# Four-layer graph network on one core: a quarter of a clamp's columns goes from GpSimd to VectorE in thirty groups of layer 2, and four degree sums go from layer 0 to layer 1

## The chip, the cores and the metric

The kernel runs on one core of a Trainium2 chip, as one launch. The metric is the device time of the launch in microseconds (us). PE is the matrix engine (TensorE; PEld is its weight load), DVE is VectorE, ACT is ScalarE, POOL is GpSimd, and SP is the engine whose queue issues the loads from memory.

## The reference, cut to what matters

There are 4096 nodes with 64 features each. The matrix `adj` has 4096 x 4096 floats (64 MB)[...], so every layer reads it again. Each of the four layers normalises `x`, computes a graph layer of the result and adds it to `x`.

```python
# layer 0: plain sum over neighbours
h = relu(layernorm(x));  x = x + relu((adj @ h) @ W.T + b)
# layer 1: hyperbolic attention
h, q, k = lorentz_linear(...)               # q and k from h
att = adj * sigmoid((2 + 2 * (qm @ k.T)) / att_scale + att_bias)
s = att @ h;  x = x + s / sqrt(clip(abs(lorentz_norm(s)), 1e-08))
# layer 2: log map between all pairs of nodes, weighted with adj / degree
deg = maximum(adj.sum(axis=1, keepdims=True), 1e-08)
log_ij = logmap(x[:, None], x[None, :])     # needs arctanh of a distance per pair
agg = einsum('ij,ijc->ic', adj / deg, log_ij)
x = x + expmap(0, agg @ weight + bias)
# layer 3: weights that decay with the rank of a neighbour, from a cumsum of the mask
x = x + w(rank) @ (h @ weight) + bias
```

Two things matter here. The degree `deg` is used only in layer 2, but it needs a sum over the whole of `adj`, which the kernel takes while earlier layers pass over it. And the distance of a pair in layer 2 is the same both ways, so it is computed once for a pair of nodes and used for both directions.

## The kernel before, in words

**Tiles.** `adj` is laid out so that one load brings a group: a tile of 128 x 2 x 512 floats (512 KB), for one row `ib` of 512 target nodes (eight rows, NB) and two chunks of 128 source nodes (sixteen groups `g` in a row, NG). Loads are issued by SP in a fixed order (`feed`, L804 to L813) into ten buffers: six of `adjp` and four of `adj01`, the latter in layers 0 and 1 only. A buffer can be loaded again when all users of its group are done with it (`left` counts them): PE for the sums, and DVE as well where it takes a degree sum.

**Order of the work.** The kernel is written as many threads (`l0_sums`, `l2_clamps`, ...), each of which says on which engine its next step runs and when its inputs are ready. `in_turn` (L733) always takes the thread that can start first by a cost model, `Pace` (L60), and emits its instruction; the order of each engine's instructions is then fixed at compile time. All instructions are issued by one helper, `InOrder` (L124), so the profile shows the line L132 for nearly everything, and groups are told apart by the names of their tiles. Threads joined by `in_steps` (L1266) run in a fixed order relative to each other: the second number of each entry says by how many steps a stage lies behind. Where `Pace` expects PE to wait 0.6 us or more, `keep_warm` (L768) puts idle matmuls of the identity with itself (`tr<-ident`) on PE.

**Layer 0.** For each group PE adds adj x h into an accumulator (`pair_sum`, L866), four passes in f32. DVE adds the group into `dg` (`degree_sums`, L890), a running sum of 128 x 2 x 512; the first group of a row is a copy. At the end of a row `after0` (L566) copies the accumulator, adds the two halves of `dg`, and PE turns `dg` into degrees by matmuls with a column of ones. In rows 1 to 6 the groups in `LEFT` (3, 7, 11, 15) are left out of this sum; they are added up in layer 1 instead, and `after1` (L591) then has four more matmuls with ones, a copy to `r_c` on ACT and an addition to `deg` on DVE. In row 0 and row 7 all sixteen groups are summed in layer 0. The last twelve groups of layer 0 alternate with the first of layer 1 (`EARLY`), and layer 1's rows 0 and 1 are run together at the start.

**Layer 1.** PE makes q k for a group (`mm<-qT,kT`), ACT the sigmoid (`sig<-mm`), DVE multiplies by `adj` (`sig<-sig,adj`), PE sums (`acc<-sig,HL`).

**Layer 2.** The work is a list of 72 groups, `work`: row `ib`, and for each column block `J` from `ib` on two halves. A group with J = ib has only pairs within one block: its first half is whole, and its second is "cut" to half of its columns. A group with J > ib is a "two": its result is used directly for row `ib` and also, transposed, for row `J`. One step for one group runs through all engines:

- PE: the product of a pair (`mm<-RT,LT` and `mm<-RB,LB`), transposes (`tr<-ident,t`), the sums `acc<-w,HA` of 128x512 for the row itself (`l2_sums`), and of 128x256 for the transposed half (`l2_sums2`).
- ACT: the square of the product into `v`, then Ln of `v` (`v<-v,minus`), the root (`t<-v`), the inverse (`v<-v`), and the log (`t<-t`).
- POOL: between square and Ln, a clamp of `v` from below, `v<-v`, 128x1024 (`l2_clamps`, L1076 to L1081). It keeps the argument of Ln, v minus a constant, positive.
- DVE: `t<-mm,t` (`l2_coshs`), `t<-t,v` (`l2_pairs`), `w<-t,adj` (`l2_weights`), and two times `w<-tr,adj` 128x512 for the transposed half (`l2_weights2`).

ACT's order in a step is: Ln(k), root(k), square(k+1), inverse(k), log(k). DVE's is: pairs(k-1), weights(k-1), cosh(k), and the two w(k-1). A thread of its own, `l2_gathers` (L1253), adds the finished transposed sums of a column block into `others` after its second half (in row 0 it is a copy on ACT, in later rows an addition on DVE); until that is done, the next block's transposed sums can't start, since they use the same accumulator. At a row's end `after2` (L633) adds `others` to the row's sum (tile `e`) and computes the row's new `x`.

**Layer 3.** Ranks are counted from the mask with bf16 matmuls, made into weights on ACT (`wt<-mm`), and used in two more passes. Nothing in it is touched.

**On POOL** there are, beside the clamps, only small powers (`ln_r<-ln_v`) and constants. In rows of layer 2 the groups of rows' work (`before2`, `after2`) run at the beginning and end of a row, between the steps.

Of the kernel before, what the change touches and what calls it, by code (L numbers as in the profile page):

```python
# [14 lines left out]
ALU = mybir.AluOpType  # L15
# [8 lines left out]
NB = N // W  # L24
CB = W // P
G = 2
NG = NC // G
LEFT = (3, 7, 11, 15)
WAIT = 0.6
EARLY = 12  # L30
BEHIND = NG - CB // G
# [18 lines left out]
B_MIN = 2.0**-22  # L50
SC = 2.0**-19
HALF = 0.25 * SC * SC
Q = 32


# [84 lines left out]
def kernel(ctx: ExitStack, tc: tile.TileContext, a: dict, out: bass.AP):  # L140
# [4 lines left out]
    pace = Pace()  # L145
    PE, DVE, ACT, POOL = (
        InOrder(tc, e, pace, name)
        for e, name in (
            (nc.tensor, "PE"), (nc.vector, "DVE"), (nc.scalar, "ACT"), (nc.gpsimd, "POOL"),
        )  # L150
    )
# [83 lines left out]
    minus = const.tile([P, 1], F32, name="minus")  # L235
    POOL.memset(minus, -HALF)
    shift = const.tile([P, 1], F32, name="shift")
# [3 lines left out]

    rbs = [const.tile([P, CB, 4, Q], F32, name=f"rb{k}") for k in range(2)]
    lbs = [const.tile([P, CB // 2, 4, Q], F32, name=f"lb{k}") for k in range(2)]
    near = const.tile([P, P], BF16, name="near")
    far = const.tile([P, Q], BF16, name="far")
    pick = const.tile([P, KH, Q], BF16, name="pick")
    spread = const.tile([P, 2, 4, NC], BF16, name="spread")

    def later_constants():
# [9 lines left out]
        def weights_of_ranks():  # L259
# [5 lines left out]
            for q in range(4):  # L265
                b = slice(q * Q, (q + 1) * Q)
                DVE.tensor_copy(far[b, :], near_f[b, b])
# [12 lines left out]
            for r in range(4):  # L280
                yield "DVE", lambda: 150.0
                b = slice(r * Q, (r + 1) * Q)
                for h in range(2):
# [63 lines left out]
    def emptied(t):  # L347
        k = [k for k in in_use if k[0] is t][0]
        in_use.remove(k)
        spare.append(k[1])  # L350
# [379 lines left out]
    def latest(*times):  # L730
        return None if None in times else max(times)
# [36 lines left out]
    def keep_warm(wait):  # L768


        if wait < WAIT or not spare or l1[0].get("dist") and "tables" not in opened or "third" in opened:
            return
# [15 lines left out]
    opened = {}  # L788
# [26 lines left out]
    def used(d):  # L815
        d["left"], d["at"] = d["left"] - 1, max(d["at"], pace.latest)

    def ready(t, more=0.0):
        return pace.ready[pace.name(t)] + more

    def arrival(d, more=0.0):
        return ready(d["adj"], more) if "adj" in d else None
# [31 lines left out]


    def group(layer, ib, g):
        degree = (g in LEFT and 0 < ib < NB - 1) == (layer == 1)
        return {"layer": layer, "ib": ib, "g": g, "degree": degree, "left": 1 + degree, "at": 0.0}

    l0 = [group(0, ib, g) for ib in range(NB) for g in range(NG)]
    l1 = [group(1, ib, g) for ib in range(2) for g in range(BEHIND)]
    l1 += [group(1, ib, g) for ib in range(2) for g in range(BEHIND, NG)]
    l1 += [group(1, ib, g) for ib in range(2, NB) for g in range(NG)]
    order = l0[: len(l0) - EARLY] + [d for pair in zip(l0[len(l0) - EARLY :], l1) for d in pair]  # L866
# [109 lines left out]
    def l1_sums():  # L976
        for pair in pairs:
# [24 lines left out]
    work = [  # L1002
        {"ib": i, "J": j, "half": s, "g": j * (CB // G) + s, "first": i == j and s == 0,
         "last": j == NB - 1 and s == CB // G - 1, "two": i < j, "cut": i == j and s == 1,
         "left": 1 + (i == j and s == 1), "at": 0.0}
        for i in range(NB) for j in range(i, NB) for s in range(CB // G)
    ]
    twos = [d for d in work if d["two"]]


    OWN = G * P

    def part(d, t):
        return t[:, :, OWN:] if d["cut"] else t
# [4 lines left out]
    def ago(items, k, n, what):  # L1019

        return items[k - n].get(what) if k >= n else 0.0
# [54 lines left out]
    def l2_clamps():  # L1076
        for d in work:
            yield "POOL", lambda: d.get("square")
            v = part(d, d["v"])
            POOL.tensor_scalar(v, v, HALF * (1.0 + 2.0**-23), None, ALU.max)  # L1080
            d["clamped"] = pace.latest  # L1081

    def l2_signs():
        for d in work:
            yield "PE", lambda: d.get("square")
            for c in range(G):
                b = slice((2 * c + 1) * Q, (2 * c + 1) * Q + 2)
                PE.matmul(
                    part(d, d["ps"])[:, c, :], LB[b, d["g"], :], RB[b, targets(d)],
                    start=False, stop=True, skip_group_check=True,  # L1090
                )
            d["signed"] = pace.latest

    def l2_first_logs():
        for d in work:
            yield "ACT", lambda: latest(d.get("clamped"), opened.get("tables"))
            v = part(d, d["v"])
            ACT.activation(v, v, AF.Ln, bias=minus)
            d["first_log"] = pace.latest
# [19 lines left out]
    def l2_coshs():  # L1119
        for d in work:  # L1120
            yield "DVE", lambda: latest(d.get("root"), d.get("signed"))
            t = part(d, d["t"])
            DVE.scalar_tensor_tensor(t, part(d, d["ps"]), 0.5 * SC, t, ALU.max, ALU.add)
            d["read"] = pace.latest
# [7 lines left out]
    def l2_pairs():  # L1132
        for d in work:
            yield "DVE", lambda: latest(d.get("log"), d.get("inverse"))
            t = part(d, d["t"])
            DVE.scalar_tensor_tensor(t, t, top, part(d, d["v"]), ALU.min, ALU.mult)
            d["paired"] = pace.latest

    def l2_weights():
        for k, d in enumerate(work):  # L1140
            yield "DVE", lambda: latest(
                opened.get("second"), d.get("paired"), arrival(d), ago(work, k, 2, "summed")
            )
            if not d["cut"]:
                d["w"] = w2["pool"].tile([P, G, W], F32, tag="w", name="w")
            DVE.tensor_mul(part(d, d["w"]), part(d, d["t"]), part(d, d["adj"]))
            d["weighed"] = pace.latest
            used(d)
# [34 lines left out]
    def l2_weights2():  # L1183
        k = -1
        for n, d in enumerate(work):
            if d["first"]:
                own = work[n + 1]
                yield "DVE", lambda: latest(
                    ready(d["tr", 0]) if ("tr", 0) in d else None, arrival(own),
                    ago(work, n + 1, 2, "summed"),  # L1190
                )
                own["w"] = w2["pool"].tile([P, G, W], F32, tag="w", name="w")
                DVE.tensor_mul(
                    own["w"][:, :, 0:OWN], d["tr", 0].rearrange("p (k j) -> p k j", j=OWN),
                    own["adj"][:, :, 0:OWN],
                )
                emptied(d["tr", 0])
                used(own)
            k += d["two"]
            for c in range(G if d["two"] else 0):  # L1200
                yield "DVE", lambda: latest(
                    ready(d["tr", c]) if ("tr", c) in d else None,
                    ready(d["adj2"]) if "adj2" in d else None, ago(twos, k, 2, "summed2"),
                )
                if c == 0:
                    d["w2"] = w2["pool"].tile([P, CB, G * P], F32, tag="w2", name="w2")
                j = (d["half"] * G + c) * P
                DVE.tensor_mul(
                    d["w2"][:, :, c * P : (c + 1) * P],
                    d["tr", c].rearrange("p (k j) -> p k j", j=P), d["adj2"][:, :, j : j + P],  # L1210
                )
                emptied(d["tr", c])
            d["weighed2"] = pace.latest
# [242 lines left out]
    def l3_sum():  # L1456
# [22 lines left out]
        if d["last"]:  # L1479
# [10 lines left out]
        ),  # L1490
        in_steps(
            (l2_first_logs(), 0, once), (l2_roots(), 0, once), (l2_squares(), -1, once), (l2_inverses(), 0, once), (l2_logs(), 0, once),
        ),
        l3_counts(),
        in_steps(
            (l2_pairs(), 1, once), (l2_weights(), 1, once),
            (l2_coshs(), 0, once), (l2_weights2(), 1, lambda d: 2 if d["two"] else 1 if d["first"] else 0),
        ),
        l2_clamps(), l2_gathers(), l3_weights(), l3_pass(), l3_masks(), l3_bias(),
        degree_sums(0, l0), degree_sums(1, l1), constants(), *later_constants(),  # L1500
    ])
# [45 lines left out]
```

## Time and profile before

| what | us |
|---|---|
| median of three runs | 1160.33 (1156.4 to 1161.47) |
| profiled execution: its time | 1154.0 |
| profiled execution: span from first to last instruction | 1152.3 |
| granted clock of PE in it | 0.992 of full speed |

| stretch of the span, us | PE busy | DVE busy | ACT busy | POOL busy | GB/s from memory |
|---|---|---|---|---|---|
| 0 to 190 (layer 0) | 168.9 | 164.0 | 77.1 | 47.2 | 371 |
| 190 to 465 (mostly layer 1) | 266.1 | 228.6 | 192.7 | 29.0 | 241 |
| 465 to 911 (layer 2) | 415.3 | 389.8 | 380.3 | 205.1 | 164 |
| 911 to 1152 (mostly layer 3) | 225.7 | 132.0 | 134.9 | 4.4 | 258 |

How to read it: a line of a timeline has the start in us, the duration, the engine, the operation with its output tile, input tiles and shape, the number of instructions joined (x4), and in brackets how long the engine was idle just before and which instruction on which engine ended that. A line of the costliest groups has the total busy time and the mean in ns after the bar, then the idle time just before these instructions and who ended it. In the chain that ended last, each line has the start, the duration and the instruction; "issue" is time for which the profile shows no wait. A line of SP's waits has the engine it waited for, then the total in us, the count and the longest. Matmuls are pipelined, so a busy PE is not PE at its peak.

### The profile page before, as it was taken

The page shows a single profiled execution, that of the slowest core. Times are in us where ns is not written, and L with a number is a line of the kernel's source. Part 1 is how long each engine was busy: PE and PEld are TensorE (multiplying, and loading weights), DVE is VectorE, ACT ScalarE, POOL GpSimd, SP SyncE. Part 2 cuts the span into 40 slices and gives each one's busy share as a digit, 9 for nine tenths or more (in the row PEclk, how much of TensorE's full clock was granted, in tenths as well). Part 3 has the DMA queues.
Part 4 walks back from the last instruction along what each step waited for, and adds up shares of the span by engine and source line. Part 5 has one row for each costly group of instructions (what it writes and reads, how often), then busy time and mean ns, then how long its engine had stood idle before and what let it go on. Part 6 is the DMA issues. An engine that isn't in the chain of part 4 may idle for free.

```text
span 1152.3 us, 15824 instructions
## 1 busy us (share of the span) xinstructions
PE 1076.0 (93%) x5496; PEld 451.4 (39%) x5496; DVE 914.3 (79%) x1473; ACT 785.0 (68%) x1286; POOL 285.7 (25%) x150
## 2 busy tenths in 40 slices
PE   6889999999999999999989989999999889999998
PEld 3234443333333333445434444444444433333332
DVE  7789898778888887697789888898999995555550
ACT  1145546676777667888888888897888664555554
POOL 3022222112100000254445444454445300000000
PEclk9899999999999999999999999999999999999999
DMA  7999999766677677534534535535355489888830
GB/s 277 388 384 395 409 387 357 293 217 204 213 261 241 222 236 249 175 122 161 183 132 168 197 110 186 179 128 187 124 201 173 153 351 369 321 317 321 319 114 10
DMA packets 77192, 271.77 MB, mean 236 GB/s; under 512 B 10040, under 2 KB 11064, under 8 KB 77112
## 3 DMA queue, kind: packets, MB, share of 16 engines
q1 hardware_dynamic: 75456, 270.57, 65.2%
q8 instruction: 43, 0.70, 0.2%
q10 hardware_dynamic: 1656, 0.20, 0.1%
q14 instruction: 37, 0.30, 0.1%
HBM read 269.68 MB, written 1.05 MB: 235 GB/s over the span
## 4 chain that ended last, share of the span: by engine, by line
PE 36%; DVE 18%; issue 17%; ACT 12%; POOL 11%; DMA 5%; ACTq 0%; POOLq 0%; DVEq 0%; SPq 0%
PE acc L132 15%; PE mm L132 13%; POOL v L132 10%; PE tr L132 8%; DMA adj<-in_adjT_dram 4%; ACT wt L132 3%; DVE w L132 2%; DVE sig L132 2%; DVE dg L132 2%; DVE t L132 2%; ACT v L132 2%; ACT sig L132 2%; ACT t L132 1%; DVE r_n L132 1%; POOL ln_r L132 1%
## 5 line engine op out<-in xcount | busy, mean ns | idle before, releaser
L132 PE MATMUL acc<-w,HA 128*65 128x256 f32 (+1 forms) x736 | 245.1, 468 | 15.9 <-DVE w L132 14.2
L132 POOL TENSOR_SCALAR v<-v 128x1024 f32<-128x1024 f32 x72 | 192.7, 2676 | 243.0 <-ACT v L132 238.8
L132 ACT ACTIVATE sig<-mm,att_b,att_a 128x1024 f32<-128x1024 f32 x128 | 148.9, 1200 | 53.7 <-PE mm L132 50.5
L132 ACT ACTIVATE wt<-mm 128x1024 uint16<-128x1024 f32 x124 | 120.2, 1020 | 85.4 <-PE mm L132 85.4
L132 DVE TENSOR_TENSOR sig<-sig,adj 128x1024 f32<-128x1024 f32 x128 | 152.6, 1220 | 28.5 <-ACT sig L132 26.6
L132 DVE TENSOR_TENSOR dg<-dg,adj 128x1024 f32<-128x1024 f32 x114 | 139.2, 1221 | 1.9 <-DMA adj<-in_adjT_dram 0.2
L132 PE MATMUL mm<-qT,kT 64*128 64x512 f32 x512 | 130.5, 623 | 5.9 <-ACT sig L132 5.5
L132 PEld LDWEIGHTS acc<-w,HA 128*65 128x65 f32 x736 | 93.4, 137 | 101.7 <-issue 48.1
L132 PE MATMUL acc<-adj,HA 128*64 128x512 f32 x512 | 123.3, 611 | 9.8 <-DMA adj<-in_adjT_dram 9.7
L132 PE MATMUL acc<-sig,HL 128*64 128x512 f32 x512 | 124.3, 608 | 1.5 <-DVE sig L132 1.4
L132 DVE SCALAR_TENSOR_TENSOR t<-mm,t 128x1024 f32<-128x1024 f32 x72 | 83.6, 1162 | 33.4 <-ACT t L132 24.7
L132 ACT ACTIVATE v<-v,minus 128x1024 f32<-128x1024 f32 x72 | 79.2, 1100 | 44.9 <-POOL v L132 44.4
L132 PE MATMUL acc<-wt,S 128*64 128x512 bf16 x496 | 99.2, 388 | 0.2 <-ACT wt L132 0.2
L132 DVE SCALAR_TENSOR_TENSOR t<-t,v 128x1024 f32<-128x1024 f32 x72 | 83.4, 1159 | 9.6 <-ACT t L132 9.6
L132 DVE TENSOR_TENSOR w<-t,adj 128x1024 f32<-128x1024 f32 x72 | 83.7, 1163 | 1.8
L132 DVE TENSOR_SCALAR RT<-adj 128x1024 bf16<-128x1024 f32 x74 | 51.2, 704 | 40.2 <-PE mm L132 39.1
L132 ACT ACTIVATE t<-t 128x1024 f32<-128x1024 f32 x72 | 72.1, 1001 | 12.4 <-DVE t L132 12.3
L132 PE MATMUL mm<-RT,LT 64*128 64x512 f32 (+1 forms) x288 | 78.5, 622 | 0.0
L132 DVE TENSOR_TENSOR w<-tr,adj 128x512 f32<-128x512 f32 x120 | 77.2, 680 | 0.0
L132 POOL TENSOR_TENSOR ln_r<-ln_v,minus_half 128x4 f32<-128x4 f32 x24 | 41.6, 1731 | 135.0 <-DVE ln_v L132 135.0
L132 ACT ACTIVATE t<-v 128x1024 f32<-128x1024 f32 x72 | 72.8, 1011 | 2.1
L132 PEld LDWEIGHTS mm<-qT,kT 64*128 64x128 f32 x512 | 43.3, 186 | 78.8 <-ACT sig L132 36.1
(214 smaller groups left out, 1407.6 us busy)
## 6 DMA issues: line engine op xcount, KB each, us to landing
adj<-in_adjT_dram SPq DMA_DIRECT2D x512, 512.0 KB, 4.6
x<-in_x_dram SPq DMA_DIRECT2D x4, 256.0 KB, 4.3
out_dram<-h SPq DMA_DIRECT2D x8, 128.0 KB, 2.0
b<-in_b_dram ACTq DMA_DIRECT2D x2, 32.0 KB
W<-in_W_dram ACTq DMA_DIRECT2D x3, 16.0 KB, 5.3
W0T<-in_W0T_dram ACTq DMA_DIRECT2D x2, 16.0 KB, 3.9
W1T<-in_W1T_dram ACTq DMA_DIRECT2D x1, 16.0 KB
W1T<-in_b_dram ACTq DMA_DIRECT2D x1, 0.2 KB
```

What stands on the lines that cost most here:

```text
L132: done = self.tc.keep_in_program_order(getattr(self.engine, op)(*args, **kw))
```

## The change

Two edits.

1. Degree sums. For row 0, the groups 4, 5, 6 and 7 (`FRONT`) are left out of the degree sum of layer 0 and summed in layer 1, as the groups in `LEFT` already are for rows 1 to 6. Row 0 of layer 1 gets a `dg` tile with it: a copy and three additions of 128x1024 on DVE, one addition of its two halves, four matmuls with ones, a copy to `r_c` on ACT and an addition to `deg`.
2. The clamp. A group of layer 2 is "shared" where its row is below 6 and its column block is at least three beyond the row, that is 10, 8, 6, 4 and 2 groups in rows 0 to 4, 30 of 72. For these POOL clamps columns 256 to 1023 (128x768), and DVE clamps columns 0 to 255 (128x256) in a new thread, `l2_clamps_v`, which stands in DVE's fixed order between cosh(k) and the two w(k-1), for group k+1. The Ln of a group then waits for both clamps.

```diff
@@ constants
 LEFT = (3, 7, 11, 15)
+FRONT = (4,5,6,7,)
...
+FLOOR = HALF * (1.0 + 2.0**-23)
+CLAMPED = 256
@@ group
-        degree = (g in LEFT and 0 < ib < NB - 1) == (layer == 1)
+        degree = (g in (LEFT if ib else FRONT) and ib < NB - 1) == (layer == 1)
@@ work
     twos = [d for d in work if d["two"]]
+    for d in work:
+        d["shared"] = d["ib"] < 6 and d["J"] >= d["ib"] + 3 and not d["cut"]
@@ l2_clamps
             yield "POOL", lambda: d.get("square")
-            v = part(d, d["v"])
-            POOL.tensor_scalar(v, v, HALF * (1.0 + 2.0**-23), None, ALU.max)
+            v = part(d, d["v"]) if not d["shared"] else d["v"].rearrange("p c i -> p (c i)")[:, CLAMPED:]
+            POOL.tensor_scalar(v, v, FLOOR, None, ALU.max)
             d["clamped"] = pace.latest
+
+    def l2_clamps_v():
+
+        for d in work:
+            yield "DVE", lambda: d.get("square")
+            if d["shared"]:
+                v = d["v"].rearrange("p c i -> p (c i)")[:, 0:CLAMPED]
+                DVE.tensor_scalar(v, v, FLOOR, None, ALU.max)
+            d["clamped_v"] = pace.latest
@@ l2_first_logs
-            yield "ACT", lambda: latest(d.get("clamped"), opened.get("tables"))
+            yield "ACT", lambda: latest(d.get("clamped"), d.get("clamped_v"), opened.get("tables"))
@@ the list of threads
-            (l2_coshs(), 0, once), (l2_weights2(), 1, lambda d: 2 if d["two"] else 1 if d["first"] else 0),
+            (l2_coshs(), 0, once), (l2_clamps_v(), -1, once), (l2_weights2(), 1, lambda d: 2 if d["two"] else 1 if d["first"] else 0),
```

Because the emission order is chosen by the cost model, the compiled order of each engine also moves. Against before, DVE has 30 clamps of 128x256 more, one copy into `dg` more and one addition less among its sums of groups, and the two small additions at the end of row 0 of layer 1; POOL has 30 clamps of 128x768 in place of 128x1024; PE has four matmuls with ones more, and 62 idle matmuls `tr<-ident` in place of 32 (seven more at the first shared step of each of rows 1 to 4, ahead of the transposed sums of block J = ib + 2, and two more in row 0); ACT has the copy to `r_c`. From the first shared step of a row on, DVE's addition into `others` stands behind `t<-t,v` of the next step, where it stood ahead of it, next to the two `w<-tr,adj`. In row 0 of layer 0 the matmuls of `after0` come one group earlier. The four moved sums stand on DVE behind the last groups of layer 0. SP issues the same 523 transfers in the same order, but the buffers it waits for are freed by PE alone where a degree sum has gone.

## The prediction

> **What bounds the kernel now.** I read the page's chain first, then the costliest groups, then the timelines of one run of equal steps in layer 2, engine by engine, and last the start. In layer 2 the chain that ended last alternates between a clamp on POOL and 3.23 us of other work, so one step takes 6.03 us. The two forms of the clamp are listed by shape.
>
> ```profile
> 624.89 2.76 POOL v L132
> 627.65 3.22 issue
> 630.92 2.77 POOL v L132
> ...
> L132 POOL TENSOR_SCALAR v<-v 128x1024 f32<-128x1024 f32 x64 | 180.4, 2818 | 222.8 <-ACT v L132 218.6 <-DVE w L132 4.2
> L132 POOL TENSOR_SCALAR v<-v 128x512 f32<-128x512 f32 x8 | 12.3, 1540 | 20.2 <-ACT v L132 20.2
> ```
>
> The loop is: clamp(k) on POOL, then on ACT Ln(k), root(k), square(k+1), then clamp(k+1). From start to start ACT takes 1.18 + 0.97 + 1.09 us, the clamp 2.77, the hand-over 0.03: 6.04. While POOL clamps, ACT does inverse and log and then waits 0.99 us for POOL. So a shorter clamp pays until something else takes 6.03 us as well. PE nearly does. The timeline of PE in the same row:
>
> ```profile
> 623.83 1.88 PE L132 MATMUL acc<-w,HA 128*65 128x512 f32 x4
> 625.64 1.13 PE L132 MATMUL mm<-RT,LT 64*128 64x512 f32 x4
> 626.71 0.40 PE L132 MATMUL mm<-RB,LB 32*128 32x512 bf16 x4
> 627.03 1.94 PE L132 MATMUL acc<-w,HA 128*65 128x256 f32 x8
> 628.81 1.04 PE L132 MATMUL tr<-ident,t 128*128 128x128 f32 x8
> 629.68 1.88 PE L132 MATMUL acc<-w,HA 128*65 128x512 f32 x4
> ...
> 639.07 1.94 PE L132 MATMUL acc<-w,HA 128*65 128x256 f32 x8 [0.27 <-DVE w L132]
> ...
> 663.19 1.94 PE L132 MATMUL acc<-w,HA 128*65 128x256 f32 x8 [0.72 <-DVE w L132]
> ...
> 670.41 0.46 PE L132 MATMUL tr<-ident,e 65*128 65x65 f32 x4 [1.31 <-DVE e L132]
> ```
>
> From 623.83 to 629.68 is one step without a wait: 5.85 us. After each row's start PE is behind and runs several steps at 5.85 while ACT and POOL run at 6.03. A step can't get shorter than 5.85, whatever the clamp does; what can be won is PE's waits.
>
> **The clamp.** POOL costs (2.77-1.49)/512 = 2.5 ns a column, so 768 columns take 2.13: 0.64 less. Thirty groups are cut (J at least ib+3: ten, eight, six, four and two in rows 0 to 4). If POOL's loop alone counted, 30 x 0.64 = 19.2 us would go. With PE's 5.85 it is the waits inside the cut stages and at their ends: 0.30+0.30+0.73 in row 0, 0.27+0.30+0.72 in row 1, 0.27+0.73, 0.70, and 0.32 in row 4: 4.6 us. At each row's end PE also waits for e (0.97, three times 1.31, 0.77). With a DVE that is ahead e moves up by about 1.2: today cosh before it waits 0.63 for ACT, and without that DVE is held only by PE's transposes. I take 0.9 + 3 x 1.2 + 0.7 = 5.2.
>
> **VectorE's share.** No row has this operation at 256 columns. A 128x128 TENSOR_SCALAR takes 0.23 and a 128x1024 one 0.68, so 256 columns are 0.30 us by these. DVE's own step is 1.14 (cosh) + 1.19 (two w) + 1.25 + 1.15 = 4.73, and 0.60 more every second step for the sum into "others": with the clamp 5.03 or 5.63, mean 5.33, under 5.85.
>
> But the clamp on DVE starts beside POOL's. The Trainium skill ("SBUF — State Buffer", Who interferes with whom) says that a DVE operation in a 2-port mode and a GpSimd operation exclude each other: the later one blocks until the first one ends. TENSOR_SCALAR from SBUF to SBUF is of that kind. DVE reaches the new instruction 0.2 us after POOL has started, so by the rule it would stand 1.9 us. The trace has both answers:
>
> ```profile
> 593.65 2.76 POOL L132 TENSOR_SCALAR v<-v 128x1024 f32<-128x1024 f32 x1 [3.96 <-ACT v L132]
> 595.71 0.73 DVE L132 TENSOR_SCALAR r_n<-r_n 128x4 f32<-128x4 f32 x1
> ...
> 600.75 2.77 POOL L132 TENSOR_SCALAR v<-v 128x1024 f32<-128x1024 f32 x1 [4.33 <-ACT v L132]
> 602.16 0.17 DVE L132 TENSOR_SCALAR ln_v<-ln_v 128x4 f32<-128x4 f32 x1
> ```
>
> The first came 2.06 us into a clamp and ended with it; the second came 1.41 in and took its usual 0.17. At 513.74 a copy (r_v<-r_i) that came 0.47 us into a clamp took 0.60 instead of 0.15, so it was let go about 0.9 in. So POOL holds DVE at its beginning (to 0.9) and its end (from about 1.9), not between. Scaled to 768 columns: to 0.7 and from 1.4. On time, DVE then stands 0.5 (a step of 5.83 in the mean, still under 5.85); late by that much, not at all. I take 0.5 where DVE is the bound, with 0 and 1.9 as ends.
>
> **Where DVE is the bound: "others".** In the compiled order of the changed kernel the sum into "others" stands behind pairs (t<-t,v), where it stood before or just behind the two w. The sums of the turned half (acc<-w 128x256) wait for it. At the first cut step of rows 1 to 4 DVE has no idle time: in row 1 its cosh ends at 613.08, then clamp 0.3 and 0.5 of standing, two w, pairs 1.25, others 0.60: 616.8 instead of 614.9. PE was there at 615.33 without a wait. It now waits 1.6 us, and this four times: +6.3 (4.9 if DVE never stands; 12.4 if it stands 1.9). The order also has seven idle matmuls at just these places; at 0.13 each (six took 0.94) they lie inside the wait. Two more in row 0 cost 0.3. In later steps others ends as PE arrives, by the same addition, so it costs nothing there. Layer 2: -4.6 - 5.2 + 6.3 + 0.3 = **-3.2 us**.
>
> **The degree sums.** In row 0 of layer 0 DVE sums all sixteen groups, and SP can't load into a buffer that DVE still needs.
>
> ```profile
> SPq L812 <- DVE dg L132: 25.4, 15, 8.8
> ...
> core 0: us, PE busy (x) PEld busy (x) DVE busy (x) ACT busy (x) POOL busy (x), PEclk, DMA share, GB/s
> 24.00:28.00 4.00, 1.08 (x4) 0.20 (x4) 3.87 (x4) 0.00 (x0) 0.00 (x0) 1.00 0.40 135
> ...
> 200.77 0.17 DVE L132 TENSOR_SCALAR lo_n<-lo_n 128x8 f32<-128x8 f32 x1 [2.23 <-ACT lo_sq L132]
> ...
> 201.86 2.36 DVE L132 TENSOR_TENSOR sig<-sig,adj 128x1024 f32<-128x1024 f32 x2 [0.48 <-ACT sig L132]
> ```
>
> The first line is SP's waits up to 80 us; the stretch from 24 to 28 shows DMA at 135 GB/s, against 410 later. Four sums less are 4 x 1.23 = 4.9 us of DVE. Groups 10 and 11 then go into buffers that PE alone frees, at about 16 instead of 18.6 and 20.1. Loads also wait for the load two before them to land, so not all comes through; following the landings group 16 arrives some 3 us sooner. I take -3.5 (ends: -1 and -4.9). No DMA is added or moved in SP's order. The same sums come back behind the last groups of layer 0: a copy and three adds, 0.69 + 3 x 1.22 = 4.4 us on DVE between 191 and 202. DVE's idle 2.23 + 0.48 there covers 2.7; the other 1.7 delay sig, and PE's sums behind it. Row 0 of layer 1 also gets four matmuls with their loads (half of a group of sixteen that took 1.89: 0.9 on a PE that is full), a 0.68 add on DVE and a 0.2 copy on ACT, both in later idle time. Layers 0 and 1: -3.5 + 1.7 + 0.9 = **-0.9 us**.
>
> **Sum.** -3.2 - 0.9 = -4.1 us on the profiled execution (span 1152.3, time 1154.0). That execution lies 6.3 us under the median of the three runs, so the change is put onto the median: 1160.3 - 4.1 = 1156.2.
>
> **Rivals.**
> *More is won.* If DVE arrives ahead at the rows' ends and "others" is not late, the 6.3 us go away, and the start keeps 4.9 without the 1.7 behind it: -4.6 - 5.2 + 0.3 - 4.9 + 0.9 = -13.5, 1147. For it: DVE idles 1.1 us in a step without others. Against: in rows 1 to 4 it has no idle time from row start to the first cut step.
> *The port makes it slower.* If the rule holds for the whole clamp, DVE stands until POOL ends. Then log, behind cosh, delays the next Ln: by the same additions two steps take 12.05 (12.06 now), nothing is won in rows 1 to 4, and PE's four waits are 3.1 each: 12.4. Row 0, whose others are on ACT, still gains 1.3 and 0.9: 12.4 - 2.2 + 0.3 - 0.9 = +9.6, 1170. It decides once DVE stands over about 1.5 us in a step. For it: the 0.73 above. Against: the 0.17.
> *It does not matter.* The shorter clamp is absorbed and the start's gain is eaten by the late sums: 1160.
>
> **Chances.** Likeliest 0.47 (own range 1152 to 1161), more won 0.25, port 0.19, no matter 0.09. About 0.5% (5.8 us) is what a measurement of this kernel can tell from no change. Faster by more, under 1154.5: the second case and a quarter of the first, 0.36. Slower by more, over 1166.1: most of the third, 0.18. The rest 0.46. The range, 1147 to 1169, leaves out the lower part of the second case and the upper of the third.
>
> **What would show it.** Right: POOL 128x768 near 2.13, steps in the cut stages of 5.85, PE without waits there but one of 1.2 to 1.7 before acc<-w 128x256 at the first cut step of rows 1 to 4; DVE v<-v 128x256 between 0.3 and 0.8; the first sixteen groups done 3 us sooner. Wrong: DVE's clamp at 2 us, PE's waits over 3, or steps under 5.8, which would mean that PE's floor is not one.

## The result, and the profile after

The changed kernel takes 1149.76 us in the median of five runs (1147.19 to 1151.13), the kernel before 1160.33 (1156.4 to 1165.79). The ratio is 0.9892, with a 95% interval of 0.9861 to 0.9923: faster by about 1.1%. The two profiled executions lie closer together: 1154.0 and 1149.76 in time, 1152.3 and 1148.0 in span. The forecast was -4.1 us, made on the profiled execution and put onto the median; why the medians differ by 10.6 us and the two traces by 4.3 is taken up below.

The costliest groups by shape, in the profile of the changed kernel:

```profile
L135 POOL TENSOR_SCALAR v<-v 128x1024 f32<-128x1024 f32 x34 | 95.2, 2799 | 133.0 <-ACT v L135 133.0
L135 POOL TENSOR_SCALAR v<-v 128x768 f32<-128x768 f32 x30 | 64.1, 2138 | 109.9 <-ACT v L135 109.9
L135 PE MATMUL tr<-ident 128*128 128x128 f32 x124 | 18.3, 292 | 0.0
L135 DVE TENSOR_SCALAR v<-v 128x256 f32<-128x256 f32 x30 | 17.5, 584 | 1.3 <-ACT v L135 1.3
```

The shorter clamp takes 2.14 us (2.13 forecast). VectorE's takes 0.58 in the mean, and its single values show why. Here are VectorE's and POOL's timelines in row 1:

```profile
610.76 0.72 DVE L135 TENSOR_SCALAR v<-v 128x256 f32<-128x256 f32 x1
...
616.60 0.28 DVE L135 TENSOR_SCALAR v<-v 128x256 f32<-128x256 f32 x1
...
621.88 0.82 DVE L135 TENSOR_SCALAR v<-v 128x256 f32<-128x256 f32 x1
...
628.14 0.41 DVE L135 TENSOR_SCALAR v<-v 128x256 f32<-128x256 f32 x1
```

```profile
610.51 2.13 POOL L135 TENSOR_SCALAR v<-v 128x768 f32<-128x768 f32 x1 [3.27 <-ACT v L135]
615.90 2.13 POOL L135 TENSOR_SCALAR v<-v 128x768 f32<-128x768 f32 x1 [3.26 <-ACT v L135]
621.73 2.13 POOL L135 TENSOR_SCALAR v<-v 128x768 f32<-128x768 f32 x1 [3.70 <-ACT v L135]
627.58 2.13 POOL L135 TENSOR_SCALAR v<-v 128x768 f32<-128x768 f32 x1 [3.72 <-ACT v L135]
```

VectorE arrives 0.25, 0.70, 0.15 and 0.56 us after POOL's start. Less the 0.28 that an unhindered one takes, it goes on 0.69, 0.70, 0.69 and 0.69 us after that start. So the first third of POOL's clamp keeps VectorE out. The latest of the 30, which came 1.28 us in, took its 0.28, while POOL's clamp took 2.24 in place of 2.13. None came later than that, so this kernel does not show what the end of POOL's clamp does; the run with half of the clamp on VectorE, below, does.

PE in the same row, from the first shared step on:

```profile
611.67 1.13 PE L135 MATMUL mm<-RT,LT 64*128 64x512 f32 x4
612.73 0.39 PE L135 MATMUL mm<-RB,LB 32*128 32x512 bf16 x4
613.06 1.83 PE L135 MATMUL tr<-ident 128*128 128x128 f32 x14
614.72 1.89 PE L135 MATMUL acc<-w,HA 128*65 128x256 f32 x8
616.45 1.04 PE L135 MATMUL tr<-ident,t 128*128 128x128 f32 x8
617.32 1.88 PE L135 MATMUL acc<-w,HA 128*65 128x512 f32 x4
...
623.17 1.88 PE L135 MATMUL acc<-w,HA 128*65 128x512 f32 x4
...
629.02 1.88 PE L135 MATMUL acc<-w,HA 128*65 128x512 f32 x4
```

No wait is left in brackets. The steps are 5.85 us (617.32, 623.17, 629.02), where before they alternated with steps that held a wait. The idle matmuls (613.06 to 614.72) stand where the sum into "others" is late: on VectorE it ends at 614.41.

PE is the engine that decides the length of a row of layer 2, so a row is best measured on it, from one row's `tr<-ident,e` to the next one's (for row 0 from 477 us on). The forecast column is the prediction's sum, row by row (with its own rounding it has -3.2 in all).

| row | before | changed | difference | forecast |
|---|---|---|---|---|
| 0 | 108.99 | 106.61 | -2.4 | -1.9 |
| 1 | 84.42 | 83.26 | -1.2 | -0.9 |
| 2 | 72.68 | 71.56 | -1.1 | -0.6 |
| 3 | 60.62 | 59.87 | -0.8 | -0.3 |
| 4 | 48.54 | 48.16 | -0.4 | +0.6 |
| 5 | 38.18 | 37.52 | -0.7 | 0 |
| sum | | | -6.5 | -3.1 |

Layers 0 and 1 end where they ended before, in these two traces: the last sigmoid starts at 474.68 and 474.66. Behind row 5 some of the gain (2.2 us) is lost: the last `wt<-mm` starts 4.2 us earlier than before, and not 6.5. PE's clock was granted at 0.57 from 906 to 910 us of the changed kernel's trace, where in the other the matching stretch had 1.00, and a load came 0.9 us after VectorE was ready for it.

### The profile page after: what moved, and what is told of

Same layout as the page of the kernel before. It is cut to its first block, busy times and chain, and to the rows that moved or that the text cites. A ratio compares the mean times of both kernels' runs of the same rounds, so it can differ in the third digit from the quotient of the medians.

```text
span 1148.0 us, 16026 instructions
## 1 busy us (share of the span) xinstructions
PE 1084.0 (94%) x5564; PEld 460.5 (40%) x5564; DVE 925.0 (81%) x1505; ACT 787.4 (69%) x1287; POOL 260.2 (23%) x150
## 4 chain that ended last, share of the span: by engine, by line
PE 51%; DVE 17%; issue 11%; ACT 9%; DMA 6%; POOL 6%; ACTq 0%; POOLq 0%; SPq 0%; DVEq 0%
PE acc L135 24%; PE mm L135 16%; PE tr L135 11%; DMA adj<-in_adjT_dram 5%; POOL v L135 5%; ACT wt L135 3%; DVE dg L135 3%; DVE sig L135 3%; DVE w L135 2%; DVE t L135 2%; ACT t L135 1%; ACT v L135 1%; ACT sig L135 1%; ACT lo_sq L135 1%; POOL lo_s L135 1%
## 5 line engine op out<-in xcount | busy, mean ns | idle before, releaser
L135 POOL TENSOR_SCALAR v<-v 128x1024 f32<-128x1024 f32 (+1 forms) x72 | 171.6, 2383 | 263.0 <-ACT v L135 263.0
L135 ACT ACTIVATE v<-mm 128x1024 f32<-128x1024 f32 x72 | 69.6, 967 | 14.4 <-PE mm L135 14.4
```

What stands on the lines that cost most here:

```text
L135: done = self.tc.keep_in_program_order(getattr(self.engine, op)(*args, **kw))
```

## The experiments

### The two parts by themselves, and the kernel before once more

The clamp alone leaves out the edit to `group`:

```diff
-        degree = (g in (LEFT if ib else FRONT) and ib < NB - 1) == (layer == 1)
+        degree = (g in LEFT and 0 < ib < NB - 1) == (layer == 1)
```

> The clamp is shared, but the degree sums stay as before. My theory: the clamp is the whole gain seen in the two traces (layer 2 was 6.4 us shorter there, layers 0 and 1 the same to 0.1 us by the last sigmoid). The steps between clamps in the shared groups stay 5.85 us, layer 2 from its first to its last clamp 427.2 us (433.6 before), ratio to before 0.994. Rival, the sums carry the other half of the measured 10.6 us, as the runs of before vary at their start: then this kernel is slower than the changed one by 4 to 6 us, ratio 0.995, and its start varies like that of before.

The sums alone share no group:

```diff
-        d["shared"] = d["ib"] < 6 and d["J"] >= d["ib"] + 3 and not d["cut"]
+        d["shared"] = d["ib"] < 0 and d["J"] >= d["ib"] + 3 and not d["cut"]
```

> The degree sums are moved, but POOL clamps all columns again. My theory: no gain, since in the trace of the changed kernel the loads of row 0 waited for each other instead of for VectorE, and the end of row 0 came 1.3 us later: ratio 0.998 to 1.002. Rival, the sums carry half of the 10.6 us: ratio 0.995 (1154).

The kernel before, with no edit:

> The kernel before, unchanged, for a second trace of it. The profiled execution of before took 1154.0, its other runs 1156 to 1166. My theory: what differs between its runs lies before 60 us, where groups 10 to 15 arrive late by differing amounts; from 336 us (sigmoid 64) to the end the two traces agree within 1 us. Rival: it is spread over all layers. Ratio 0.997 to 1.003.

Measured, each against the kernel before:

| kernel | median, us | ratio | 95% interval |
|---|---|---|---|
| clamp alone | 1155.66 | 0.9938 | 0.9914 to 0.9961 |
| sums alone | 1158.88 | 0.9965 | 0.9941 to 0.9990 |
| before again | 1161.27 | 0.9998 | 0.9978 to 1.0017 |
| both (the changed kernel) | 1149.76 | 0.9892 | 0.9861 to 0.9923 |

Both parts gain, and together they make the change's ratio within its interval (0.9938 x 0.9965 = 0.990). So the theory that the clamp is the whole gain is wrong: the sums bring 0.1 to 0.6%, which the two traces did not show. The clamp's part is as expected: 7 us, with layer 2 from first to last clamp at 428.3 us in that trace (427.2 expected; 433.6 before).

The second trace of before shows what a single execution hides. The span is 1157.9 there, not 1152.3. Up to sigmoid 64 it is 4.2 us behind, of which 3.1 come by 85 us. By the last sigmoid 2.5 of them are left, and behind 930 us another 3.1 are added, where its granted clock was 0.5 from 932.5 to 939.3 us. So the expectation that the two agree within 1 us from sigmoid 64 on is missed. Over 35 runs of the kernel before, the time goes with the mean granted clock: 14 runs with less than 0.983 took 1164.0 us in the mean, the other 21 took 1160.1. The profiled execution of before had 0.992 and was shorter than all of them. The traces differ by less than the medians (4.3 us against 10.6) because this one execution lay 6.3 us under the median of its kernel, and that of the changed kernel is its median. Against the second trace of before, the changed kernel's span is 9.9 us shorter. The clock explains a part of this spread; the rest stays open.

Where the clock falls can be read from the granted clock. First the kernel before, then the clamp alone, in stretches of 4 us from 56 us on (PE, PEld, DVE, ACT, POOL, then PE's clock, the DMA share and GB/s):

```profile
core 0: us, PE busy (x) PEld busy (x) DVE busy (x) ACT busy (x) POOL busy (x), PEclk, DMA share, GB/s
56.00:60.00 4.00, 1.63 (x8) 0.27 (x4) 1.65 (x4) 1.95 (x10) 1.85 (x1) 1.00 1.03 410
60.00:64.00 4.00, 3.32 (x20) 1.72 (x20) 3.83 (x5) 1.16 (x2) 2.03 (x13) 1.00 1.04 402
64.00:68.00 4.00, 4.00 (x28) 2.54 (x28) 3.08 (x7) 3.69 (x21) 0.00 (x0) 1.00 1.00 385
```

```profile
56.00:60.00 4.00, 2.75 (x14) 0.67 (x10) 1.31 (x4) 2.90 (x14) 0.73 (x1) 1.00 1.03 410
60.00:64.00 4.00, 2.21 (x8) 0.84 (x8) 3.07 (x4) 0.58 (x1) 3.16 (x13) 0.60 1.02 408
64.00:68.00 4.00, 4.00 (x14) 2.08 (x12) 2.56 (x4) 1.15 (x4) 0.00 (x0) 0.50 1.00 366
...
72.00:76.00 4.00, 4.00 (x11) 1.32 (x13) 3.64 (x10) 0.42 (x1) 0.21 (x1) 0.50 0.02 9
```

In layers 0 and 1 these two kernels have the same instructions in the same order, and yet the second runs at half clock from 60.8 to 77.9 us: from the copy of row 1's accumulator to that of row 2 it takes 31.3 us, and before 24.1. Near 60 us PE waits for the tile HL, layer 1's features of row 0, which VectorE makes and PE has to transpose. The first line is from the kernel before, the second from the clamp alone, the third from the sums alone:

```profile
60.68 0.60 PE L132 MATMUL tr<-ident,HL 128*64 128x128 f32 x4 [3.04 <-DVE HL L132]
...
61.80 1.03 PE L135 MATMUL tr<-ident,HL 128*64 128x128 f32 x4 [3.04 <-DVE HL L135]
...
63.68 1.03 PE L135 MATMUL tr<-ident,HL 128*64 128x128 f32 x4 [2.41 <-DVE HL L135]
```

The wait is 3.04 us in the first two, and the clock fell during it in one of them. With the moved sums it is 2.41 us, and in the trace of the sums alone the clock fell during it as well.

### "others" ahead of pairs

The list of threads decides ties, and l2_gathers stood behind VectorE's fixed order. Moved ahead of it, the addition into "others" is emitted between cosh and the two w again:

```diff
-        l3_counts(),
+        l3_counts(), l2_gathers(),
...
-        l2_clamps(), l2_gathers(), l3_weights(), l3_pass(), l3_masks(), l3_bias(),
+        l2_clamps(), l3_weights(), l3_pass(), l3_masks(), l3_bias(),
```

> The changed kernel, but the sum into others goes first where it is ready together with pairs, so VectorE adds it between cosh and the two w, ahead of pairs. My theory: the idle matmuls of 1.66 us and the wait that they cover at the first shared step of rows 1 to 4 are due to the late others, and PE has no other slack there: each of these four steps falls from 7.46 to 5.85 us of PE, layer 2 gets 6.4 us shorter, time 1143, ratio to before 0.984 to 0.987. Rival, VectorE's order is the bound (its clamp now comes 0.6 us later and holds the next Ln): no gain over the changed kernel or up to 3 us slower, ratio 0.989 to 0.992.

Measured: 1144.84 us, ratio 0.9853 (0.9824 to 0.9882). PE at the first shared step of row 1 of this kernel:

```profile
609.50 1.88 PE L135 MATMUL acc<-w,HA 128*65 128x512 f32 x4
611.30 1.13 PE L135 MATMUL mm<-RT,LT 64*128 64x512 f32 x4
612.37 0.40 PE L135 MATMUL mm<-RB,LB 32*128 32x512 bf16 x4
612.69 1.94 PE L135 MATMUL acc<-w,HA 128*65 128x256 f32 x8
614.47 1.04 PE L135 MATMUL tr<-ident,t 128*128 128x128 f32 x8
615.34 1.88 PE L135 MATMUL acc<-w,HA 128*65 128x512 f32 x4
```

The idle matmuls are gone, and the sums follow at once: the step from 609.50 to 615.34 takes 5.84 us. Rows 1 to 4 take 81.64, 69.95, 58.25 and 47.01 us, that is 1.62, 1.61, 1.62 and 1.15 less than in the changed kernel. So the late addition was the cause of the four stalls, with the idle matmuls that came with it, and nothing else was ready to take their place. With its twin below, which has idle matmuls in another place, it is the fastest kernel of this study. Its time from first to last clamp is only 2.5 us shorter, because the last clamps of row 7 come later in its order; up to clamp 66 it is 5.9 us shorter.

### No clamp on VectorE, and half of it

In the first of these, VectorE clamps nothing:

```diff
-            if d["shared"]:
+            if False:
```

> The changed kernel without VectorE's clamp: columns 0 to 255 of the shared groups are not clamped by anyone, POOL still takes 768. It leaves out that part of the computation. In its compiled order others stands ahead of the two w again. My theory, PE is the bound in these steps and VectorE's clamp with its standing (0.58 us in the mean) costs nothing: from the first clamp to the last 424.7 us as with others first, steps of 5.85. Rival, VectorE's clamp and its standing cost up to 0.5 us in each of 30 steps: 410 to 420 us.

In the second, built on "others" first, VectorE clamps twice as much:

```diff
-CLAMPED = 256
+CLAMPED = 512
```

> The kernel with others first, VectorE clamps 512 of the 1024 columns. POOL's clamp falls to 1.49 us, so the loop over POOL would allow 4.75 us a step. My theory: PE's 5.85 us is the floor, the steps stay 5.85 and layer 2 from first to last clamp stays 424.7 us within 1 us (VectorE stands to 0.5 us of POOL's clamp, its step is 5.6 to 5.8 us). Rival, POOL's loop is still the bound: steps of 5.2 to 5.4 us, 412 us. Second rival, VectorE becomes the bound: steps of 5.9 to 6.2 us, 427 to 433 us.

Measured, single executions of 1145.82 and 1147.49 us. From first to last clamp they take 424.6 and 422.0 us, where 424.7 was expected of each. That the first hits is chance: up to clamp 66 it is 3.2 us longer than "others" first, with stretches at a lower clock in between, and row 7, whose last groups come in another order, gives as much back. Rows 1 to 4 on PE tell more:

| row | others first | no clamp on VectorE | half on VectorE |
|---|---|---|---|
| 1 | 81.64 | 81.64 | 81.64 |
| 2 | 69.95 | 71.19 | 69.95 |
| 3 | 58.25 | 58.25 | 58.25 |
| 4 | 47.01 | 47.77 | 46.74 |

With POOL's clamp at 2.13 us or, at its shortest, 1.49, and with VectorE's at nothing, 0.53 or 0.62 us in the mean, rows 1 and 3 agree to 0.01 us. PE is what they wait for: a shorter clamp than the change's has nothing to win there, and VectorE's clamp costs nothing. (Rows 2 and 4 without VectorE's clamp hold two stretches, 680 to 688 and 812 to 816 us, at a granted clock of 0.79 and 0.57. In that kernel the sum into "others" stands right behind the two w in row 1, not ahead of them, and is in time there too.)

The second kernel also shows the end of POOL's clamp. VectorE's first two clamps of row 1, and POOL's beside them:

```profile
615.25 0.41 DVE L135 TENSOR_SCALAR v<-v 128x512 f32<-128x512 f32 x1
...
620.30 0.85 DVE L135 TENSOR_SCALAR v<-v 128x512 f32<-128x512 f32 x1
```

```profile
614.39 1.73 POOL L135 TENSOR_SCALAR v<-v 128x512 f32<-128x512 f32 x1 [3.27 <-ACT v L135]
619.39 1.48 POOL L135 TENSOR_SCALAR v<-v 128x512 f32<-128x512 f32 x1 [3.27 <-ACT v L135]
```

The first came 0.86 us into POOL's clamp and took its usual 0.41, and POOL's took 1.73 in place of 1.49. The second came 0.91 us in, took 0.85 and ended 0.28 us after POOL's. All 14 that came 0.91 us in or later did so.

### The wait for HL filled with idle matmuls

`transposed` gets a count of idle matmuls, which run ahead of the transposes of HL in row 0, where PE would wait. First 22 of them, on the kernel before and on "others" first:

```diff
-    def turned_to(srcs, k, to):
+    def turned_to(srcs, k, to, idle=0):
...
         ps = bank()
+        for _ in range(idle):
+            tc.keep_in_program_order(nc.tensor.matmul(ps[:, 0:P], ident, ident, start=True, stop=True))
...
-        yield from transposed(hl, D, hlT[0:D, :])
+        yield from transposed(hl, D, hlT[0:D, :], 0 if ib else 22)
```

> The kernel before, with 22 idle matmuls of the identity ahead of the four transposes of HL of row 0, into the 3.04 us in which PE waits for HL near 60 us; nothing else moves. They take 2.6 us by the rate of those in layer 2 (14 took 1.66). My theory: that wait is what makes the granted clock fall to half near 62 us in some runs (8 to 15 us at half clock in two of six traces, 2.7 us in a third), and the moved sums gain because they shorten it to 2.41 us. With it filled the clock does not fall there: more than half of the runs have a mean clock of 0.9875 or more (4 of 35 for the kernel before), ratio 0.995 to 0.997. Rival: the fall has another cause (the loads, or chance): clocks and time as before, ratio 0.999 to 1.002.

> The kernel with others first, and with the same 22 idle matmuls. The wait there is 2.41 us, so they reach 0.2 us past it. My theory: the runs at a clock of 0.981 to 0.984 (2 of 6 without them, 1150 to 1151) go away, the rest is as without them: 1144, ratio 0.984 to 0.986. Rival: they cost 1 us and mend nothing, ratio 0.986.

Each matmul turned out to be two instructions, so the 22 took 5.18 us and made PE about 2 us late. With that they measured 0.9973 (0.9955 to 0.9991) and 0.9865 (0.9840 to 0.9889). Only 4 of the 12 runs on the kernel before had a clock of 0.9875 or more, where over half were expected, but none of the 17 runs of the two was under 0.983. The next three have 11 on the kernel before, and 9 on the sums alone and on "others" first, with the same edit otherwise:

> The kernel before with 11 idle matmuls instead of 22 ahead of HL's transposes. The 22 took 5.18 us and not 2.6 (each is two instructions of 0.118), so they delayed PE by about 2 us; 11 take 2.6 and fit into the wait of 3.04. My theory: no clock fall near 62 us, no delay: ratio 0.994 to 0.997, and no run with a mean clock under 0.980 (before: 5 of 52). Rival, the clock falls near 62 us are not what the moved sums change: ratio 0.998 to 1.001.

> The moved sums alone, with 9 idle matmuls (2.1 us) in the wait of 2.41 us. My theory, the sums gain by fewer clock falls near 62 us: with the wait filled in both, the sums bring nothing more, ratio to the kernel before within 0.002 of the one of before with 11 idle matmuls. Rival, the sums gain by themselves (earlier loads): 3 to 5 us faster than that kernel, ratio 0.990 to 0.993.

> Others first, with 9 idle matmuls (2.1 us, inside the wait of 2.41 us). My theory: 1143.5, ratio 0.982 to 0.985, no run over 1148. Rival: as with others first alone, 1145 with runs up to 1151, ratio 0.985.

Measured: 0.9966 (0.9940 to 0.9991), 0.9946 (0.9922 to 0.9971) and 0.9853 (0.9813 to 0.9893). The timeline of PE in the kernel before with 11, and then its granted clock:

```profile
59.41 2.72 PE L358 MATMUL tr<-ident 128*128 128x128 f32 x22
62.38 0.60 PE L132 MATMUL tr<-ident,HL 128*64 128x128 f32 x4 [0.26 <-DVE HL L132]
```

```profile
60.00:64.00 4.00, 3.75 (x29) 2.57 (x27) 3.07 (x4) 0.69 (x2) 3.75 (x13) 1.00 1.03 410
64.00:68.00 4.00, 4.00 (x30) 3.05 (x32) 3.15 (x4) 2.73 (x13) 0.00 (x0) 1.00 1.03 385
```

None of the five traces with the wait filled has a fall between 56 and 98 us. Over all runs, the number with a mean clock under 0.983 (a run's mean does not tell where the clock fell; only the traces do):

| kernels | runs | under 0.983 |
|---|---|---|
| before | 75 | 30 |
| the clamp alone | 6 | 2 |
| with the moved sums (changed, sums alone, others first) | 23 | 5 |
| with the wait filled (five kernels) | 47 | 1 |

So the wait for HL is what lets the clock fall there: with nothing else changed, idle matmuls in it gain 0.3% on the kernel before, and of 24 such runs none is at a low clock, against 16 of 40 of the kernel before beside them. How the moved sums gain is not settled. With the wait filled on both sides they still bring 0.0020, which lies at the edge of one expectation and under the other, and the intervals overlap. By themselves they leave 4 of 12 runs under 0.983, against 14 of 35 of the kernel before beside them, so that they gain by sparing falls of the clock is not shown. On "others" first, where the sums are moved already, filling the wait brings nothing that can be told (0.9853 both), and one run still took 1151.01 us: there the rival held.

## Why the prediction was right, and where it was not

The measured median, 1149.76, lies inside the range (1147 to 1169), but it is below the likeliest case's own range (1152 to 1161). The kernel is faster by more than 0.5%, to which 0.36 was given and 0.46 to "within 0.5%". It lies nearer to the case in which more is won (1147), but not for that case's reasons: "others" was late, and the start brought nothing.

In the two traces the forecast of -4.1 us meets a difference of -4.3, and that is luck. Rows 0 to 5 of layer 2 gave 6.5 us where 3.2 were forecast, layers 0 and 1 gave nothing where 0.9 was, and 2.2 were lost behind them where nothing was.

- *PE's floor of 5.85 us* held. All the waits in the shared stages (4.6 us) went, and no step of PE became shorter. The two kernels with other shares of the clamp confirm it.
- *The waits for e* went as well: 0.97 + 3 x 1.31 + 0.77 = 5.7 us, where 5.2 were taken. In their place PE waits 0.25 us for `columns` in each row.
- *The first shared steps* lost 1.66 us each in rows 1 to 4, where 1.6 were forecast. But the seven idle matmuls there took 0.24 us each, where the prediction has 0.13 ("six took 0.94") and puts them inside the wait: the six that it counted are instructions, and each of these matmuls is two. In row 1 the sum into "others" ends at 614.41, and in the trace of before PE follows what it waits for 0.05 us later. So, by an estimate from these, the late sum cost 1.40 us and the idle matmuls that ran past it 0.26. The two more in row 0 and what goes with them cost 0.5 (0.3 forecast). The run with "others" first, where both are gone, shows that the late sum was the cause and the largest fault of the change. (The term's two ends do not come out of the prediction's own additions, which give 4.4 and 12.0 us and not 4.9 and 12.4; nothing hangs on that.)
- *The port.* Standing to 0.7 us of a 768-column clamp was forecast and is what the traces show, to 0.01 us. VectorE stood 0.30 us in the mean (0.58 less 0.28), where 0.5 was taken. The second part of the forecast, standing again from 1.4 us to the end, met no clamp of this kernel; with 512 columns the end does hold VectorE. The rule of the Trainium skill ("SBUF — State Buffer", Who interferes with whom), by which the later one of the two is blocked until the first one ends, would have the clamps shown above take 1.7 to 2.3 us; the longest of all took 0.83. Where page and measurement differ, the measurement decides. The rival that made the kernel slower fell with it.
- *What the sum for layer 2 lacked* is 3.3 us. Over rows 0 to 5 PE's idle gaps fell by 11.5 us (9.8 forecast: small waits at the rows' starts and in row 5, which has no shared group, shrank too), its idle matmuls rose by 7.2 (6.6 forecast), and the rest of its time, in which the work is the same, fell by 2.1 (nothing forecast). A part of this last is that a wait costs PE more than its own length: in the trace of before the step with the wait of 0.30 at 567.04 took 6.22 us and the one ahead of it 5.85, so 0.07 more. From 505 us to the end of row 5 PE has 14 fewer waits of over 0.15 us (23 in place of 37); by this one step they would make 1.0 us, an estimate. The other half stays open.
- *The start, -3.5 us, did not come.* SP's waits up to 80 us in the trace of the changed kernel:

```profile
SPq L815 <- DMA adj<-in_adjT_dram: 24.3, 12, 5.2
SPq L815 <- DVE dg L135: 17.6, 15, 4.2
SPq L815 <- PE acc L135: 8.1, 7, 2.4
```

  The wait for other loads in the trace of the kernel before:

```profile
SPq L812 <- DMA adj<-in_adjT_dram: 16.6, 12, 2.8
```

  The waits for VectorE fell from 25.4 to 17.6 us, and those for other loads rose from 16.6 to 24.3. Group 12 lands 3.4 us sooner than before (24.8 for 28.1), but the loads up to group 16 follow each other: groups 12, 14 and 16 are each issued within 0.1 us of the landing of the one two before, and group 14 took 9.6 us to land in place of 5.4. Group 16 landed at 37.8 us in the mean of the five traces without the moved sums and at 37.7 in that of the eight with them. The first copy of an accumulator starts at 38.1 and 37.7 us by the same count, 0.4 us apart, and single traces of either kind differ by more than that. The step that failed is "following the landings group 16 arrives some 3 us sooner": I had seen the wait for earlier loads and charged too little for it. Why group 14 took so long stays open.
- *The late sums* cost 2.0 us at the end of layer 0 (from the copy of row 6's accumulator to row 7's, 35.7 us before and 37.7 after), where 1.7 were forecast, but by another way: they hold buffers, and PE waits 2.7 us for loads (0.6 before). Layer 1 then gave it back, which was not forecast: between 205 and 345 us its `mm<-qT,kT` wait 1.1 us for `sig` in place of 4.6. The four matmuls more can be read by themselves: at the end of row 0 of layer 1, from `tr<-twice,e` to the next `acc<-sig,HL`, PE takes 1.04 us before and 1.87 with them, 0.83 more (0.9 forecast). By the last sigmoid the traces agree.
- *Put onto the median.* The forecast took the difference of one execution and added it to the median of others. The prediction had seen that this execution lay 6.3 us under the median, and took the difference as the same for both. It was not: the second trace of before is 5.6 us longer than the first, in part by falls of the clock that the first did not have. The 0.1 to 0.6% that the sums bring in the medians are not in the two traces, and no step of the prediction could see them.

## What to carry to other kernels

A shorter instruction on a side engine is worth only what the engine behind it waits for; read that from the waits of the engine with the longest step, and count for each wait its length and the refill behind it. When an instruction is added to an engine without slack, see what the order puts behind it: here a 0.6 us addition, one place too late, cost 1.6 us four times, and moving it took 6.0 us out of rows 1 to 4. Before a difference of half a per cent is forecast from one profiled execution, look at how far other executions of the same kernel lie from it, and where their granted clock falls.

## What the runs showed of the hardware

- PE's granted clock fell to 0.5 during waits of 3.04 and 2.41 us near 60 us, in some traces and not in others. It fell 1.7 to 2.9 us after the wait had begun (second trace of before, the clamp alone, the sums alone, half of the clamp on VectorE). The Trainium skill ("TensorE: Matmul & The Clock Gate", What's actually happening) has the clock halve after an idle window of about 3.4 us that runs freely. That a wait's effect varies from run to run fits a free-running window; that 2.41 us suffice is less than the page says. It also has the full clock return after some 3.4 us of work, and in one trace (the second of before) it returned 3.3 us after the wait; in three others (the clamp alone, the sums alone, half of the clamp on VectorE) it stayed at 0.5 for 13 to 16 us after it, though PE was busy throughout, as the clamp alone's stretches from 64 us on show above.
- A clamp on POOL keeps VectorE's clamp out at its beginning and at its end, and not between. Of 2.13 us (768 columns) it is the first 0.69. Of 1.49 us (512 columns) it is the first 0.48, since VectorE's clamp of 0.41 that came 0.15 us in took 0.74, and then what follows from 0.91 us on: those that came 0.50 to 0.90 us in took 0.41 or 0.42, and those that came later stood until POOL's had ended. The reverse showed too: where VectorE's clamp ran between 0.70 and 1.31 us, POOL's took 1.57 to 1.78 us in place of 1.49.
